# A graph network's first layer loads further ahead, scatters and copies later; its norms are regrouped

## The chip, the cores and the metric

The kernel runs on one core of a Trainium2 chip. The core has five engines that work side by side: TensorE (PE, matrix products and transposes; PEld is its weight load), VectorE (DVE), ScalarE (ACT), GpSimd (POOL) and SyncE (SP, which here only issues transfers). Sixteen DMA engines move data between DRAM and on-chip memory; a transfer is issued by an engine's queue, and gathers and scatters by index (DMA_INDIRECT) are all issued by POOL. The metric is the device time of one execution in microseconds (us); lower is better.

## The reference

A graph of N = 6250 nodes with 64 features (D) and 206250 edges, sorted by destination, each node with a loop edge to itself as its last one. Padded, there are 6272 nodes, 128 × 49.

```python
h = relu(layernorm(x))
msg  = relu(concat([h[dst], edge_attr_16]) @ W1 + b1)
aggr = segment_sum(msg, dst) / maximum(count, 1)
x = x + relu(aggr + h @ Wres + bres)           # layer 0
h = relu(layernorm(x))
for Wq, Wk, Wv, We, Ws, bq, bk, bv, bs, H in layers:     # three attention layers, 2, 2 and 1 heads
    kj = (h @ Wk + bk)[src] + edge_attr_32 @ We
    a  = segment_softmax(sum((h @ Wq + bq)[dst] * kj) / sqrt(C), dst)
    vj = (h @ Wv + bv)[src] + edge_attr_32 @ We
    h  = segment_sum(a * vj, dst) + h @ Ws + bs     # prelu after the first two
return x + h
```

## The kernel before

**Tiling.** Nodes are sorted by their number of edges and cut into NB = 49 blocks of 128, a node per partition; block b has room for CAP[b] edges a node (66, 46, 44, and so on down to 22), and every node in it has at least LEAST[b]. `full` tells, for the columns between LEAST and CAP, whether the node has such an edge. A block's work is then dense: partitions are nodes, columns are edges.

**Setup (L114 to L381).** The destinations are loaded in rows (`prev`, `cur`), x as `xs` (128 × 49 × 64), the sources `sf` are turned to the order of edges and written to DRAM as `srcs` (L222 to L236). A search (L184 to L271) finds each node's first edge and its count: a first pass over runs, seven gathers of the rows that matter (L213), `look_f` casts of them (L240), comparisons on DVE (L195) and on ACT (L200). A counting sort by count (L274 to L313, one-hot products) gives `at_i`, the first edge of each node in sorted order, and `num_i`, the node's number (L315 to L321). Beside this, x is normed in seven groups of LG = 7 blocks (L329 to L361): on DVE the mean (L336, L337), on POOL the subtraction (L339), on ACT the square, on DVE the variance (L343, L344), on ACT the root (L345), on DVE the reciprocal (L346), on POOL the product (L347), then PE transposes (L352), ACT's relu into `hT` (L355), and a product with `wn` (L358). POOL copies x beside it (L360), and SP writes rows of 192 numbers to the DRAM table `tabx` (L361): minus the message's part of the node, that part plus the residual product, and x itself. After at_i come `no`, `full` (41 instructions at L374) and `lack`, on DVE and POOL, which also check that the graph fits CAP and LEAST.

**Layer 0 (L461 to L617).** For block b, POOL gathers the node rows of tabx (`load_x`), the 16 edge features of all its edges (`load_e`, into a pool of four buffers), the sources (`load_src`) and the 32 edge features (`load_ea`), which SP then writes to the array `ean` for the attention. `load_src` is followed by an ACT copy of the block's last source column into `ends` (L490), for the check that the last edge of each node is its loop. `messages` (L499 to L540): PE transposes the features (`turn`, L508), ACT copies them (`eT`, L509), PE multiplies (`pm`, L518), DVE takes the maximum with the node's part into `msg` (L521, L531), multiplies the optional columns by `full`, and adds the columns up in a tree (L539). `finish` (L542 to L586) works on groups of FIN0 = 8, 8, 8, 8, 8, 4, 3 and 2 blocks: mean, residual, the norm of the new x (sum, subtraction, square, sum on DVE; the root on ACT, L570; reciprocal and product on DVE), transposes (L577), relu (`ht`, L579), the product with Wq, Wk, Wv, Ws (`po`, L584), and ACT's copy to `rows` (L586). `put` scatters a block's key and value rows to the DRAM table `tab` (L453).

**The order on POOL is written by hand** in that loop (L593 to L617); POOL issues one instruction after the other, and one that waits holds all behind it. Three blocks are loaded ahead; turn b issues `load_e(b + 3)`, a put, `load_x(b + 3)`, `load_src(b)`, a put, `load_ea(b)`. The puts are of a group whose last block is at least two turns back. The other engines' order comes from a scheduler that follows the same program.

**Loop check and attention.** After layer 0, L384 to L395 form `no_loop` from `ends` and sum the checks into `nbad_i`; an If (L397) on it chooses the attention (L620 to L758) or a general version that is not executed here. The attention fetches one indirect gather for each edge column of each block (`kv`, 4836 in three layers).

Of the kernel before, what the change touches and what calls it, by code (L numbers as in the profile page):

```python
# [97 lines left out]
def gnn_kernel(ctx: ExitStack, tc: tile.TileContext, x, src_t, dst_t, dst_row, ea16, ea32, eaT16, eaT32, w, out):  # L98
# [12 lines left out]
    bad = cp.tile([P, 5], F32, name="bad")  # L111
    k = ctx.enter_context(Kept(tc))

    with tc.tile_pool(name="chk", bufs=1) as p, tc.tile_pool(name="chk2", bufs=2) as p2, \  # L114
# [14 lines left out]
        nc.sync.dma_start(xs, x.rearrange("(p b) f -> p b f", b=NB))  # L129
        sf = p.tile([P, T], I32, name="sf")  # L130
# [20 lines left out]
        def iota(n, mult, pattern=None):  # L151
            i = p.tile([P, n], I32, name="iota_i", bufs=2)
            nc.gpsimd.iota(i, pattern=pattern or [[1, n]], base=0, channel_multiplier=mult)
            f = p.tile([P, n], F32, name=f"iota{n}_{mult}")
            nc.gpsimd.tensor_copy(f, i)
            return f
# [3 lines left out]
        col = iota(P, 0)  # L160
# [5 lines left out]
        cap = p.tile([P, NB], F32, name="cap")  # L166
        least = p.tile([P, NB], F32, name="least")
# [3 lines left out]
        nc.gpsimd.tensor_copy(cap, k.cap)  # L171
        nc.gpsimd.memset(cap[64:, 0:1], float(CAP0[64]))
        nc.gpsimd.memset(cap[32:64, 0:1], float(CAP0[32]))
# [9 lines left out]
        nc.vector.tensor_copy(first, prev.rearrange("w (c e) -> w c e", e=RUN)[:, :, 0])  # L183
        pb = pp.tile([P, WR, P], F32, name="pb")  # L184
# [26 lines left out]
        for g in range(NG0):  # L211
# [4 lines left out]
            got.append(t)  # L216

        nc.vector.memset(bad, 0.0)
        fall = p.tile([NW, WE], BF16, name="fall")
        nc.vector.tensor_tensor(fall, prev, cur, op=OP.is_gt)  # L220

# [16 lines left out]
        for g in range(NG0):  # L238
            f = p2.tile([P, LOOK], F32, name="look_f", bufs=3)
            (nc.gpsimd.tensor_copy if g else nc.scalar.copy)(f, got[g])  # L240
            for i in range(SG + (g == NG0 - 1)):
# [29 lines left out]
        nc.vector.tensor_scalar(cls, cls, -float(LOW), float(CLS - 1), op0=OP.add, op1=OP.min)  # L271

# [51 lines left out]

        wn = p.tile([D + 1, 2 * D], F32, name="wn")
        nc.gpsimd.tensor_scalar(wn[:, :D], w0[:, :D], -1.0, 0.0, op0=OP.mult, op1=OP.add)
        nc.gpsimd.tensor_add(wn[:, D:], w0[:, :D], w0[:, D:])
        LG = 7
        to_tab = tabx.rearrange("(p b) f -> p b f", b=NB)  # L329
        for g0 in range(0, NB, LG):  # L330
            g1 = g0 + LG
            n = LG
            rx = wp.tile([P, LG, 3 * D], F32, name="rx")
            xg = xs[:, g0:g1]
            m = wp.tile([P, LG], F32, name="ln_m")
            nc.vector.tensor_reduce(m[:, :n], xg, axis=AX.X, op=OP.add)  # L336
# [968 lines left out]
```

## Time and profile before

| | us |
|---|---|
| median of 3 runs (lowest, highest) | 6730.41 (6730.25, 6735.94) |
| profiled execution | 6732.95 |
| its span | 6731.2 |
| setup, until the first gather of layer 0 | 123.4 |
| layer 0, until the first gather of the attention | 454.3 |
| attention | 6153.5 |
| POOL, DVE, PE, ACT busy | 4927.7, 3127.9, 1914.8, 345.5 |

The span is cut at two of POOL's gathers: `e<-in_ea_dram,at_i` for the first block, and the first `kv<-tab,src`. In a timeline row, what stands in brackets is the idle time of the engine before that instruction and what ended it. A row of the waits is engine, line, what was waited for, total us, number of times, longest. Engines wait for each other by semaphores, and the profile infers from these what released an instruction. An engine that is idle but isn't the one that ends a stage costs nothing.

### The profile page before, as it was taken

To read this page: it belongs to the slowest core of one execution; us is meant where nothing else is said; L and a number is where in the kernel's file an instruction comes from. 1 tells how busy PE (TensorE), PEld (TensorE's weight loads), DVE (VectorE), ACT (ScalarE), POOL (GpSimd) and SP (SyncE) were. 2 spreads that over 40 slices of the span, in tenths; PEclk is the share of its full clock that TensorE was granted. 3 is DMA by queue.
4 is the path that set the end of the run, shared out by engine and by line. 5 is a ranking of instruction groups with operands and counts; after the bars stand their busy time and mean duration, and the time that the engine had idled before them with its cause. 6 is when DMAs were issued, how large, how long until landed. Compare 5 with 4: busy or idle time off the path is not lost. (4 is left out here: it accounts for less than half of the span.)

```text
span 6731.2 us, 26890 instructions
## 1 busy us (share of the span) xinstructions
PE 1914.8 (28%) x4808; PEld 1135.6 (17%) x4808; DVE 3127.9 (46%) x5986; ACT 345.5 (5%) x998; POOL 4927.7 (73%) x5264
## 2 busy tenths in 40 slices
PE   4663232333333332222222222222222222222221
PEld 3442111111111111111111111111111111111110
DVE  7763444444444444444444444444444344444444
ACT  3110000000000000000000000000000000000000
POOL 4556777777777776777777777776777777777776
PEclk9765555555555555555555555555555555555555
DMA  4553232333232322222222222222222222222221
GB/s 144 183 175 122 81 87 79 84 84 84 82 87 81 84 82 60 67 69 66 68 69 68 68 70 67 69 68 64 64 63 68 63 66 66 66 64 67 63 65 55
DMA packets 227799, 535.37 MB, mean 80 GB/s; under 512 B 90199, under 2 KB 106685, under 8 KB 226519
## 3 DMA queue, kind: packets, MB, share of 16 engines
q0 software_dynamic: 172736, 374.78, 19.6%
q1 hardware_dynamic: 52790, 156.27, 7.0%
q10 hardware_dynamic: 2090, 2.48, 0.1%
q14 instruction: 142, 1.16, 0.1%
q8 instruction: 41, 0.67, 0.0%
HBM read 459.32 MB, written 73.87 MB: 79 GB/s over the span
## 5 line engine op out<-in xcount | busy, mean ns | idle before, releaser
L447 POOL DMA_INDIRECT kv<-tab,src x4836 | 4561.7, 943 | 1518.6 <-issue 1410.4
L688 DVE TENSOR_TENSOR kv<-kv,pe 128x1024 f32<-128x1024 f32 (+6 forms) x669 | 745.0, 1114 | 2321.1 <-DMA kv<-tab,src 2152.6
L682 PE MATMUL pe<-wblk,ea 128*128 128x256 f32 x1736 | 901.4, 669 | 3046.8 <-DVE kv L688 2747.1
L682 PEld LDWEIGHTS pe<-wblk,ea 128*128 128x128 f32 x1736 | 505.7, 323 | 3420.6 <-DVE kv L688 2967.0
L682 PE MATMUL pe<-wblk,eaT 128*128 128x256 f32 x868 | 451.4, 668 | 1224.9 <-DVE kv L688 1160.8
L721 DVE TENSOR_REDUCE some<-kv 128x64 f32<-128x512 f32 (+6 forms) x690 | 610.6, 922 | 0.1
L687 DVE CAST src<-kv 128x8 int32<-128x8 f32 (+5 forms) x223 | 41.0, 184 | 1092.5 <-DMA kv<-tab,src 1041.6
L682 PEld LDWEIGHTS pe<-wblk,eaT 128*128 128x128 f32 x868 | 252.1, 322 | 1383.1 <-DVE kv L688 1273.3
L694 DVE TENSOR_TENSOR prod<-kv,more 128x512 f32<-128x512 f32 (+6 forms) x690 | 423.7, 628 | 0.8
L695 DVE TENSOR_REDUCE al<-prod 128x16 f32<-128x512 f32 (+8 forms) x690 | 422.9, 627 | 0.7
L717 DVE TENSOR_TENSOR kv<-kv,more 128x512 f32<-128x512 f32 (+6 forms) x690 | 416.7, 627 | 0.0
L706 ACT ACTIVATE more<-al,m 128x33 f32<-128x33 f32 (+22 forms) x245 | 71.7, 293 | 3189.0 <-DVE m L704 3185.8
L518 PE MATMUL pm<-w0blk,eT 64*128 64x256 f32 x868 | 192.2, 564 | 37.0 <-DVE msg L521 20.0
L659 PE MATMUL turn<-ident,ea 128*128 128x128 f32 x434 | 124.9, 432 | 77.5 <-ACT eaT L660 70.8
L453 POOL DMA_INDIRECT tab<-rows,num_i x49 | 54.5, 1112 | 117.5 <-ACT rows L586 97.9
L539 DVE TENSOR_TENSOR msg<-msg 128x960 f32<-128x960 f32 (+19 forms) x224 | 137.4, 617 | 0.8
L518 PEld LDWEIGHTS pm<-w0blk,eT 64*128 64x128 f32 x868 | 120.3, 276 | 89.6 <-DVE msg L521 25.7
L521 DVE TENSOR_TENSOR msg<-pm,rx 128x1024 f32<-128x1024 f32 x76 | 92.8, 1221 | 77.4 <-PE pm L518 72.0
L447 POOL DMA_INDIRECT e<-in_ea_dram,at_i x98 | 103.8, 1059 | 33.8 <-issue 22.2
L738 PE MATMUL po<-ws,ht 65*128 65x256 f32 x196 | 109.2, 661 | 11.5 <-ACT ht L736 11.5
L674 ACT COPY more<-rows 128x64 f32<-128x64 f32 x147 | 31.6, 216 | 1516.3 <-DVE kv L717 1507.9
L659 PEld LDWEIGHTS turn<-ident,ea 128*128 128x128 f32 x434 | 80.2, 217 | 139.1 <-ACT eaT L660 125.9
(183 smaller groups left out, 1442.8 us busy)
## 6 DMA issues: line engine op xcount, KB each, us to landing
kv<-tab,src POOLq DMA_INDIRECT x4836, 2.5
ea<-eat SPq DMA_DIRECT2D x26, 576.0 KB
ea<-eat SPq DMA_DIRECT2D x24, 512.0 KB
ea<-eat SPq DMA_DIRECT2D x16, 640.0 KB
ean<-e SPq DMA_DIRECT2D x13, 576.0 KB
ea<-ean SPq DMA_DIRECT2D x13, 576.0 KB
eat<-eaT SPq DMA_DIRECT2D x13, 576.0 KB
ea<-eat SPq DMA_DIRECT2D x16, 448.0 KB
```

What stands on the lines that cost most here:

```text
L447: return nc.gpsimd.indirect_dma_start(out=out, out_offset=None, in_=table, in_offset=bass.IndirectOffsetOnAxis(ap=idx, axis=0))
L518: nc.tensor.matmul(pm[:, r, u].rearrange("p j f -> p (j f)"), eT[h, t0 // 8 + u, :], k.w0blk[h, :], start=True, stop=True)
L521: nc.vector.tensor_tensor(msg[:, t0:t0 + 16], pm.rearrange("p r u j f -> p (r u j) f"), nega[:, None, :].to_broadcast([P, 16, D]), op=OP.max)
L539: nc.vector.tensor_add(to, msg[:, :h], msg[:, c - h:c])
L659: nc.tensor.transpose(ps[:, i - i0, :], t[:, i, :], ident)
L682: nc.tensor.matmul(pe[:, 4 * g:4 * g + 4].rearrange("p j f -> p (j f)"), ea[:, t0 // 4 + g, :], k.wblk[l], start=True, stop=True)
L688: nc.vector.tensor_add(pair(kv[:, :m, :2 * D]), pair(kv[:, :m, :2 * D]), pe[:, :m, None, :].to_broadcast([P, m, 2, D]))
L694: nc.vector.tensor_mul(prod[:, :n], kv[:, :n, :D], q[:, None, :].to_broadcast([P, n, D]))
L695: nc.vector.tensor_reduce(al[:, :H, t0:t0 + n].rearrange("p h j -> p j h"), prod[:, :n].rearrange("p j (h c) -> p j h c", h=H), axis=AX.X, ...
L717: nc.vector.tensor_mul(v.rearrange("p j (h c) -> p j h c", h=H), v.rearrange("p j (h c) -> p j h c", h=H), ex[:, :H, t0:t0 + n].rearrange( ...
L721: nc.vector.tensor_reduce(some[:, i, :], v.rearrange("p j f -> p f j"), axis=AX.X, op=OP.add)
L738: nc.tensor.matmul(po, ht[:, :P], k.ws[l + 1], start=True, stop=True)
```

## The change

- **x into tabx.** A DMA issued by POOL ahead of everything else copies x straight into the last 64 columns of tabx; the tile `rx` of the setup then holds 128 columns, and SP writes pieces of 512 B a row, in groups of eight blocks instead of seven.
- **The norm of x in whole passes.** One mean reduce over all of x on DVE, before the counts; four subtractions on POOL and four squares on ACT; one variance reduce on DVE, one root on ACT, one reciprocal; six products on POOL, which stand between the `look_f` casts. Transposes, relu and product follow the comparisons on ACT, before the counting sort. `k.ht` is used for the relu.
- **Moved.** The reduce of `fall` and the copies of weights to `ws` come earlier in the setup. `no`, `full` and `lack` leave the setup for the head of layer 0, and are all on DVE; the tile `cap` goes, and two comparisons for the narrower lanes of block 0 take its place.
- **Order in layer 0.** AHEAD: `load_e` and `load_x` run four blocks ahead, not three; e16 has five buffers and one of its own for block 0, e32 three and one of its own. LATE: puts are of groups at least four turns back, and the copies to `ends` (now `last`) of block b − 4 follow the gather of block b. LATER: `load_ea` is for block b − 6. The remaining copies, six `load_ea` and the last puts come after the loop, a `load_ea` with up to two puts.
- **messages.** Where at most three columns are optional, they are left out of the tree and added to the sum by multiply-add with their column of `full`.
- **finish.** The norm's subtraction, square and sum on DVE go. ACT squares each block with the mean as bias and sums it up in the same instruction, eight for a group; DVE forms (x + m) · v block by block. `h0` has one buffer, `sq` two.

```diff
         nc.sync.dma_start(xs, x.rearrange("(p b) f -> p b f", b=NB))
+        nc.gpsimd.dma_start(tabx[:, 2 * D:], x)
         sf = p.tile([P, T], I32, name="sf")
...
-        cap = p.tile([P, NB], F32, name="cap")
         for t, values in ((k.cap, CAP), (least, LEAST)):
...
                 nc.gpsimd.memset(t[:, i:j], float(v))
-        nc.gpsimd.tensor_copy(cap, k.cap)
-        nc.gpsimd.memset(cap[64:, 0:1], float(CAP0[64]))
-        nc.gpsimd.memset(cap[32:64, 0:1], float(CAP0[32]))
         going = p.tile([P, CLS, NB], BF16, name="going")
...
         nc.vector.tensor_copy(first, prev.rearrange("w (c e) -> w c e", e=RUN)[:, :, 0])
+        mean = p.tile([P, NB], F32, name="mean")
+        var = p.tile([P, NB], F32, name="var")
+        hn = p.tile([P, NB, D], F32, name="hn")
+        sq = k.rows.rearrange("p b f -> p (b f)")[:, 2 * WE + NG0 * LOOK:2 * WE + NG0 * LOOK + NB * D] \
+            .rearrange("p (b f) -> p b f", f=D)
+        part4 = [slice(0, 13), slice(13, 25), slice(25, 37), slice(37, 49)]
+        nc.vector.tensor_reduce(mean, xs, axis=AX.X, op=OP.add)
+        nc.vector.tensor_scalar(mean, mean, 1.0 / D, None, op0=OP.mult)
+        for s in part4:
+            nc.gpsimd.tensor_sub(hn[:, s], xs[:, s], mean[:, s, None].to_broadcast([P, s.stop - s.start, D]))
+            nc.scalar.activation(sq[:, s], hn[:, s], AF.Square)
         pb = pp.tile([P, WR, P], F32, name="pb")
...
             got.append(t)
+        nc.vector.tensor_reduce(var, sq, axis=AX.X, op=OP.add)
+        nc.vector.tensor_scalar(var, var, 1.0 / D, 1e-5, op0=OP.mult, op1=OP.add)
+        nc.scalar.activation(var, var, AF.Sqrt)
+        nc.vector.reciprocal(var, var)
...
         nc.vector.tensor_tensor(fall, prev, cur, op=OP.is_gt)
+        nc.vector.tensor_reduce(bad[:NW, 0:1], fall, axis=AX.X, op=OP.max)
...
             (nc.gpsimd.tensor_copy if g else nc.scalar.copy)(f, got[g])
+            if g:
+                s = slice(8 * (g - 1), min(NB, 8 * g)) if g < 6 else slice(40, NB)
+                nc.gpsimd.tensor_mul(hn[:, s], hn[:, s], var[:, s, None].to_broadcast([P, s.stop - s.start, D]))
             for i in range(SG + (g == NG0 - 1)):
...
         nc.vector.tensor_scalar(cls, cls, -float(LOW), float(CLS - 1), op0=OP.add, op1=OP.min)
+        wn = p.tile([D + 1, 2 * D], F32, name="wn")
+        nc.gpsimd.tensor_scalar(wn[:, :D], w0[:, :D], -1.0, 0.0, op0=OP.mult, op1=OP.add)
+        nc.gpsimd.tensor_add(wn[:, D:], w0[:, :D], w0[:, D:])
+        for t in k.ht:
+            nc.gpsimd.memset(t[D:D + 1, :], 1.0)
+        LG = 8
+        to_tab = tabx.rearrange("(p b) f -> p b f", b=NB)
+        for g0 in range(0, NB, LG):
+            g1 = min(NB, g0 + LG)
+            rx = wp.tile([P, LG, 2 * D], F32, name="rx")
+            for b0 in range(g0, g1, 4):
+                nb = min(4, g1 - b0)
+                pt = psum.tile([D, 4 * P], F32, name="pr_t")
+                for b in range(nb):
+                    nc.tensor.transpose(pt[:, b * P:(b + 1) * P], hn[:, b0 + b, :], ident)
+                ht = k.ht[b0 // 4 % 2]
+                nc.scalar.activation(ht[:D, :nb * P], pt[:, :nb * P], AF.Relu)
+                po = psum.tile([P, 4, 2 * D], F32, name="pr_o")
+                for b in range(nb):
+                    nc.tensor.matmul(po[:, b, :], ht[:, b * P:(b + 1) * P], wn, start=True, stop=True)
+                nc.scalar.copy(rx[:, b0 - g0:b0 - g0 + nb], po[:, :nb])
+            nc.sync.dma_start(to_tab[:, g0:g1, :2 * D], rx[:, :g1 - g0])
+        for l in range(LAYERS):
+            nc.gpsimd.tensor_copy(k.ws[l][:, :D], wl[l][:, 3 * D:])
+            nc.gpsimd.tensor_scalar(k.ws[l][:, D:2 * D], wl[l][:, :D], float(D // HEADS[l]) ** -0.5, 0.0, op0=OP.mult,
+                                    op1=OP.add)
+            nc.gpsimd.tensor_copy(k.ws[l][:, 2 * D:], wl[l][:, D:3 * D])
...
-        LG = 7
...
-            rx = wp.tile([P, LG, 3 * D], F32, name="rx")
-            xg = xs[:, g0:g1]
-            m = wp.tile([P, LG], F32, name="ln_m")
-            nc.vector.tensor_reduce(m[:, :n], xg, axis=AX.X, op=OP.add)
-            nc.vector.tensor_scalar(m[:, :n], m[:, :n], 1.0 / D, None, op0=OP.mult)
-            hn = wp.tile([P, LG, D], F32, name="hn0")
-            nc.gpsimd.tensor_sub(hn[:, :n], xg, m[:, :n, None].to_broadcast([P, n, D]))
-            sq = wp.tile([P, LG, D], F32, name="ln_sq")
-            nc.scalar.activation(sq[:, :n], hn[:, :n], AF.Square)
-            v = wp.tile([P, LG], F32, name="ln_v")
-            nc.vector.tensor_reduce(v[:, :n], sq[:, :n], axis=AX.X, op=OP.add)
-            nc.vector.tensor_scalar(v[:, :n], v[:, :n], 1.0 / D, 1e-5, op0=OP.mult, op1=OP.add)
-            nc.scalar.activation(v[:, :n], v[:, :n], AF.Sqrt)
-            nc.vector.reciprocal(v[:, :n], v[:, :n])
-            nc.gpsimd.tensor_mul(hn[:, :n], hn[:, :n], v[:, :n, None].to_broadcast([P, n, D]))
...
-            nc.gpsimd.tensor_copy(rx[:, :, 2 * D:], xg)
-            nc.sync.dma_start(to_tab[:, g0:g1], rx)
         nc.gpsimd.tensor_copy(k.rows[:, :, 4 * D:4 * D + 1], place[:, :, None])
...
-        nc.vector.tensor_reduce(bad[:NW, 0:1], fall, axis=AX.X, op=OP.max)
-        no = p.tile([P, 2, NB], F32, name="no")
-        nc.vector.tensor_tensor(no[:, 0], k.deg, cap, op=OP.is_gt)
-        nc.vector.tensor_tensor(no[:, 1], k.deg, least, op=OP.is_lt)
-        nc.vector.tensor_reduce(bad[:, 1:3], no, axis=AX.X, op=OP.add)
-        for b in range(NB):
-            if CAP[b] > LEAST[b]:
-                s = slice(WOFF[b], WOFF[b + 1])
-                nc.vector.tensor_scalar(k.full[:, s], col[:, LEAST[b]:CAP[b]], k.deg[:, b:b + 1], None, op0=OP.is_lt)
-        nc.gpsimd.tensor_scalar(k.lack, k.full, BIG, -BIG, op0=OP.mult, op1=OP.add)
...
-    layer0(tc, ea16, ea32, ident, tabx, srcs, k)
+    layer0(tc, ea16, ea32, ident, tabx, srcs, k, col, least, bad)
     with tc.tile_pool(name="nb", bufs=1) as p, tc.tile_pool(name="nbp", bufs=1, space=PSUM) as pp:
...
-def layer0(tc, ea16, ea32, ident, tabx, srcs, k):
+def layer0(tc, ea16, ea32, ident, tabx, srcs, k, col, least, bad):
     nc = tc.nc
...
         nc.vector.memset(eps, 1e-5)
-        for t in k.ht:
-            nc.vector.memset(t[D:D + 1, :], 1.0)
+        no = wp.tile([P, 2, NB], F32, name="no", bufs=1)
+        nc.vector.tensor_tensor(no[:, 0], k.deg, k.cap, op=OP.is_gt)
+        nc.vector.tensor_tensor(no[:, 1], k.deg, least, op=OP.is_lt)
+        nc.vector.tensor_single_scalar(no[64:, 0, 0:1], k.deg[64:, 0:1], float(CAP0[64]), op=OP.is_gt)
+        nc.vector.tensor_single_scalar(no[32:64, 0, 0:1], k.deg[32:64, 0:1], float(CAP0[32]), op=OP.is_gt)
+        nc.vector.tensor_reduce(bad[:, 1:3], no, axis=AX.X, op=OP.add)
+        for b in range(NB):
+            if CAP[b] > LEAST[b]:
+                s = slice(WOFF[b], WOFF[b + 1])
+                nc.vector.tensor_scalar(k.full[:, s], col[:, LEAST[b]:CAP[b]], k.deg[:, b:b + 1], None, op0=OP.is_lt)
+        nc.vector.tensor_scalar(k.lack, k.full, BIG, -BIG, op0=OP.mult, op1=OP.add)
         st = {}
...
             n = up(CAP[b], 8)
-            t = st["e16", b] = gp.tile([P, up(MAXC, 8) * 16], F32, name="e16")
+            t = st["e16", b] = gp.tile([P, n * 16], F32, name="e16_0", bufs=1) if b == 0 else \
+                gp.tile([P, up(CAP[1], 8) * 16], F32, name="e16", bufs=5)
             pick(nc, t[:, :n * 16], ea16, k.at_i[:, b:b + 1])
...
             pick(nc, k.src[0][:, OFF[b]:OFF[b + 1]], srcs[:, None], k.at_i[:, b:b + 1])
+        def last(b):
             nc.scalar.copy(k.ends[:, b:b + 1], k.src[0][:, OFF[b + 1] - 1:OFF[b + 1]])
...
             at = k.at_i[:, b:b + 1]
-            t = gp.tile([P, max(G32) * P], F32, name="e32", bufs=3)
+            t = gp.tile([P, G32[0] * P], F32, name="e32_0", bufs=1) if b == 0 else \
+                gp.tile([P, G32[1] * P], F32, name="e32", bufs=3)
             pick(nc, t[:, :G32[b] * P], ea32, at)
...
                                                 nega[:, None, :].to_broadcast([P, m, D]), op=OP.max)
-            if c > LEAST[b]:
+            few = range(LEAST[b], c) if c - LEAST[b] <= 3 else ()
+            if c > LEAST[b] and not few:
                 nc.vector.tensor_mul(msg[:, LEAST[b]:c], msg[:, LEAST[b]:c],
                                      k.full[:, WOFF[b]:WOFF[b + 1], None].to_broadcast([P, c - LEAST[b], D]))
+            sum_ = st["sum", g][:, b - first[g]:b - first[g] + 1, :]
+            c -= len(few)
             while c > 1:
                 h = c // 2
-                to = msg[:, :h] if c > 2 else st["sum", g][:, b - first[g]:b - first[g] + 1, :]
-                nc.vector.tensor_add(to, msg[:, :h], msg[:, c - h:c])
+                nc.vector.tensor_add(msg[:, :h] if c > 2 else sum_, msg[:, :h], msg[:, c - h:c])
                 c -= h
+            for i, j in enumerate(few):
+                w = WOFF[b] + i
+                nc.vector.scalar_tensor_tensor(sum_, msg[:, j:j + 1], k.full[:, w:w + 1], sum_, op0=OP.mult, op1=OP.add)
...
             nc.vector.reciprocal(c[:, :n], c[:, :n])
-            h = wp.tile([P, GN, D], F32, name="h0")
+            h = wp.tile([P, GN, D], F32, name="h0", bufs=1)
             nc.vector.tensor_mul(h[:, :n], s[:, :n], wide(c))
...
             nc.vector.tensor_reduce(m[:, :n], x, axis=AX.X, op=OP.add)
-            nc.vector.tensor_scalar(m[:, :n], m[:, :n], 1.0 / D, None, op0=OP.mult)
-            nc.vector.tensor_sub(h[:, :n], x, wide(m))
-            sq = wp.tile([P, GN, D], F32, name="sq", bufs=1)
-            nc.vector.tensor_mul(sq[:, :n], h[:, :n], h[:, :n])
+            nc.vector.tensor_scalar(m[:, :n], m[:, :n], -1.0 / D, None, op0=OP.mult)
             v = wp.tile([P, GN], F32, name="v0")
-            nc.vector.tensor_reduce(v[:, :n], sq[:, :n], axis=AX.X, op=OP.add)
+            for i in range(n):
+                sq = wp.tile([P, D], F32, name="sq")
+                nc.scalar.activation(sq, x[:, i], AF.Square, bias=m[:, i:i + 1], accum_out=v[:, i:i + 1])
             nc.scalar.activation(v[:, :n], v[:, :n], AF.Sqrt, bias=eps[:, 0:1], scale=1.0 / D)
             nc.vector.reciprocal(v[:, :n], v[:, :n])
-            nc.vector.tensor_mul(h[:, :n], h[:, :n], wide(v))
+            for i in range(n):
+                nc.vector.tensor_scalar(h[:, i], x[:, i], m[:, i:i + 1], v[:, i:i + 1], op0=OP.add, op1=OP.mult)
             for i0 in range(0, n, 4):
...
         wait = []
+        AHEAD, LATE, LATER = 4, 4, 6
         with tc.manual_schedule(engines={mybir.EngineType.Pool}):
-            for b in range(3):
+            for b in range(AHEAD):
                 load_e(b)
...
             for b in range(NB):
-                old = [r for r, at in wait if at <= b - 2][:2]
+                old = [r for r, at in wait if at <= b - LATE][:2]
                 wait = wait[len(old):]
-                if b + 3 < NB:
-                    load_e(b + 3)
+                if b + AHEAD < NB:
+                    load_e(b + AHEAD)
                 if old:
                     put(old.pop(0))
-                if b + 3 < NB:
-                    load_x(b + 3)
+                if b + AHEAD < NB:
+                    load_x(b + AHEAD)
                 load_src(b)
...
                     put(old.pop(0))
-                load_ea(b)
+                if b >= LATER:
+                    load_ea(b - LATER)
+                if b >= LATE:
+                    last(b - LATE)
                 messages(b)
...
                     wait += [(r, b) for r in range(first[g], first[g] + FIN0[g])]
-        for r, _ in wait:
-            put(r)
+            for b in range(NB - LATE, NB):
+                last(b)
+            rest = list(range(NB - LATER, NB))
+            while rest or wait:
+                if rest:
+                    load_ea(rest.pop(0))
+                for r, _ in wait[:2]:
+                    put(r)
+                wait = wait[2:]
```

## The prediction

> **What bounds the kernel now.** I read the windows by stage first: the setup until block 0's edge gather is issued (123.4), layer 0 until the first attention gather (577.7), and the attention. After the two bounds come duration, busy time of PE, PEld, DVE, ACT and POOL (instruction counts in brackets), granted clock, DMA share and GB/s.
>
> ```profile
> 0.00:123.40 123.40, 51.56 (x229) 42.60 (x229) 95.41 (x212) 48.83 (x110) 50.74 (x134) 1.00 0.31 98
> 123.40:577.70 454.30, 289.74 (x1247) 184.03 (x1247) 303.10 (x615) 65.17 (x175) 265.49 (x245) 0.69 0.54 180
> 577.70:6731.20 6153.50, 1573.47 (x3332) 908.97 (x3332) 2729.41 (x5159) 231.54 (x714) 4611.43 (x4885) 0.51 0.25 72
> ```
>
> The attention is 91% of the span. Its groups say that POOL issues 4836 gathers, each 943 ns with some 300 ns ("issue" idle) after it: 4836 × 1.24 = 6011 us. None of its code is edited, so the 6153.5 us stay; the change can move only the first 577.7. Next, the waits of layer 0 (window 123 to 572: total us, times, longest):
>
> ```profile
> ACT ends L490 <- DMA src<-srcs,at_i: 197.0, 41, 8.9
> POOL tab L453 <- ACT rows L586: 97.9, 6, 29.5
> DVE msg L521 <- PE pm L518: 72.0, 32, 6.2
> ```
>
> ACT stands 197 us on the loop-check copies (L490), and POOL, which issues every gather of the stage, 97.9 us on six table scatters (L453). POOL's timeline shows where: start, duration, and in brackets the idle time before and its releaser.
>
> ```profile
> 123.44 1.02 POOL L447 DMA_INDIRECT e<-in_ea_dram,at_i  x1 [1.52 <-PE pr_o L358]
> 127.90 0.95 POOL L447 DMA_INDIRECT rx<-tabx,num_i  x1 [3.45 <-DMA tabx<-rx]
> 221.72 1.03 POOL L453 DMA_INDIRECT tab<-rows,num_i  x1 [29.51 <-ACT rows L586]
> 295.51 1.02 POOL L453 DMA_INDIRECT tab<-rows,num_i  x1 [18.08 <-ACT rows L586]
> ...
> 499.10 1.15 POOL L453 DMA_INDIRECT tab<-rows,num_i  x1 [9.28 <-ACT rows L586]
> ...
> 577.77 0.99 POOL L447 DMA_INDIRECT kv<-tab,src  x1 [6.00 <-issue]
> ```
>
> Each row with L586 is the first scatter of a group of eight blocks. The group's last ACT copy is late, POOL stands, no gather is issued, and the next blocks start late. The groups between have stalls of 17.27 and 14.04. DVE's timeline gives the setup's end:
>
> ```profile
> 113.22 0.20 DVE L316 SCALAR_TENSOR_TENSOR at_i<-join 128x49 int32<-128x49 f32 x1
> ...
> 115.64 5.83 DVE L374 TENSOR_SCALAR full<-iota,deg 128x22 f32<-128x22 f32 x41
> ```
>
> The list that gathers need (at_i) is there at 113.4, but the first gather is issued at 123.44, and block 0's rows of tabx come at 127.90.
>
> **The setup.** DVE's rows L336, L343 and the small ones of norm run between the counts and the permutation. From 60 to 113 I add five L343 reduces (0.62 each, the profile's row at 112.69) and three L336 (0.62): 5.0, some 1.5 of small rows of 0.16 to 0.2, and waits for POOL and ACT of about 1.2. DVE's rows beside POOL's norm work run long there too (L309, val, is 1.58 to 2.31 for one form; three such stretches give some 3): about 9.5 leave. One whole reduce is added before the counts. By 7 pieces at the pitch of a pair of the L336 rows (1.14 for two, so 0.57) it is 4.0, against pieces that filled gaps there: the counts end 1.5 later, with POOL's four subtractions (7 × 0.92 by L339 = 6.4) before the seven gathers at 27.9. Net, at_i comes 8 earlier (bounds 4 and 11).
>
> Behind at_i, POOL now waits for pr_o (L358), for `lack`, and for tabx. Norm's product ends long before, `full` (5.83) and `lack` stand at the head of layer 0 on DVE, and there the first e and x gathers cover them (first gather 123.44, first message 133.77: 10.3). So e(0) follows at_i by 1.7 (num_i, num, one queue step) instead of 10.1: −8.4. x(0), the one that was issued last, gains the 3.45 wait as well, but the DVE needs block 0's e and x together. I take −8 −8.4 = −16.4, bounds −9 to −23 (all of 127.90 − 105).
>
> **The copy of x into tabx** is one DMA on POOL, ahead of all its setup: 6272 rows of 256 B, DRAM to DRAM. No row of this trace has POOL issue a plain DMA, so I bound it by the indirect ones:
>
> ```profile
> 636.52 0.94 POOL L447 DMA_INDIRECT kv<-tab,src  x1 [0.30 <-issue]
> 641.37 0.87 POOL L447 DMA_INDIRECT kv<-tab,src  x1 [0.30 <-issue]
> ```
>
> The second gather writes 32 lanes, the first 128: 0.07 more for 96 more rows, 0.73 ns per row. So 6272 rows are 0.87 + 4.5 = 5.4 us at the one end, and 49 × 0.94 = 46 us at the other, if every 128 rows cost a whole issue. POOL's setup before the data arrive is busy 6.4 in 2 to 18, so 5.4 is covered by the 10 us that it idles until x lands at 18.4; 46 is not: the seven run gathers go from 29.7 to 61, +31. I take 5.4, as the rows within one instruction are the nearer likeness to one instruction.
>
> What it moves competes: in 2 to 18 the DMA engines are 94% busy. In 658 to 700 the share is 0.22 of 16 engines for 34 gathers of 128 rows, so a row of 528 B takes 0.22 × 16 × 42 / 4352 = 34 ns, and 6272 rows are 213 us on one engine, 13.3 on sixteen. x (18.4) shares the engines with it and lands between 0 and 13.3 later. I take +8, somewhat past the middle because the copy and the rows it delays are issued at the same time; all of the setup behind moves with it.
>
> A rule speaks against the copy: the Trainium skill, page "DMA: Bandwidth & Descriptors", section Specifications, says that a transfer of at least 512 B is the minimum for line rate, and that below it the engine reads, modifies and writes. No trace here shows rows of 256 B beside rows of 512 B. By that rule a 256-B row could cost up to twice the 34 ns that the gathers' row shows, an estimate from that page: 27 us of all engines, and the whole sum would stand near −26 instead of −45.
>
> **Layer 0, group 0** (blocks 0 to 7). From the first message (133.77) to the first scatter (221.72) are 88 us. DVE is busy 60.25 of the 71.8 between 133.7 and 205.5, and the stall of 29.51 on POOL covers the group's finish. ACT no longer holds block b's transposed copies (eT) behind block b's own src gather: the copy `ends` moves four blocks behind. With its 11.5 idle halved to gone, DVE ends the group 6 to 11.5 earlier, and a fourth block ahead changes nothing here because DVE, not the gathers, sets it. The finish keeps its length (below). I take −11, bounds 0 and −15.
>
> **Groups 1 to 4.** The distance between first scatters is 73.8, 71.3, 68.5 and 63.7, sum 277.3; each holds 40 issues on POOL (8 each of e, x, src, ea and put) in 54.4 to 55.7, so 1.36 apiece with their gaps, and a stall of 18.1, 17.3, 14.0 or 9.3. In the new order the put of a group stands four blocks behind its last block, not two. But it does not follow that the stall vanishes: the finish's squares are now ACT instructions, eight a group, and in ACT's order they stand behind eT(b+3) and the ends copy of b+3's turn, as the square root stood behind eT(b+4) before. They come with e(b+3) landed, and the first put is only two POOL issues behind that turn's. From the issue that ACT waits for I count: landing 3.0 (2.5 from the src issue at 136.65 to the copy at 139.17, and a little for busier queues), copy 0.2, eT 0.85 (L509), eight squares of 64 columns at 0.35 = 3 (an L490 copy of one column is 0.19, L570 0.30; bounds 1.6 to 3.3), root 0.3 (L570), root to last needed rows 6.3 (215.16 to 221.44, L570 to L586); sum 13.6, less three issues of 1.36 that POOL does meanwhile: 9.6 stall. A cycle is then 40 × 1.36 + 9.6 = 64, four are 257: −20 against 277.3. The bounds are a stall of 18 left (0) and none (−58.7 for the four stalls).
>
> Finish on DVE gives up a subtraction, a product and a reduce (0.68 each for 8 blocks) and takes eight `tensor_scalar` of 64 columns for the product. That is −2 + 1 on an engine that waits; zero, with ±1 per group. `few` replaces a product over up to three columns per block by up to three multiply-adds of 64: three at 0.2 against one at 0.25 to 0.35; ±0.2 × 49 = ±10 on DVE, covered by its waits of 72 us for PE (L521) in groups 1 to 7; without that cover up to +10.
>
> **The tail.** From group 4's first put to the first attention gather are 577.77 − 499.10 = 78.7. It loses the stalls 9.75 and 6.78 in part, and the six late e32 gathers come last: e(48) of them is the last issue, lands in 4, its copy to `ean` on SP takes about 2.5, and the check follows (573.57 to 577.77, 4.2, L387, unchanged). SP's `ean` copies, moved six blocks later, wait behind nothing else on SP's queue. I count 73.4: −5, bounds −15 and +5.
>
> **Sum.** −16.4 + 8 − 11 − 20 − 5 = −44.4, say −45 against the profiled execution's 6732.95, which stands 2.5 above the median of 6730.41: 6688, in terms of the median **6686**.
>
> **Rivals.** *A, POOL needs 46 us to issue the copy.* For it: each indirect issue costs 0.94. Against: the 32-lane rows. +31.6 while the +8 of the engines is then hidden: −45 + 23 = −22, 6708. *B, the puts stop waiting.* For it: four blocks is twice two. Against: ACT's order above. The remaining 38 of the four stalls go, and 10 of the tail: 6638. *C, slower:* the issue of the copy holds POOL for over 67 us (10.7 ns a row; the seven gathers then start behind it, and every us more is a us of span). At that price the gain of 45 is used up, at 85 us the time is 6748. Against: no row is over 7.3 ns a row. *D, the stalls only move:* landing of src and squares keep the 18, the engines' share takes the 8; setup −8, no more: 6722, within 0.2%.
>
> **How the numbers follow.** Forecast 0.62, A 0.16, B 0.13, D 0.05, C 0.04. A measurement of this kernel can tell about 0.2%, 13.5 us, from no change. Faster: forecast, A and B, less a little: 0.90; same 0.05; slower 0.05. The forecast alone, with setup and engine bounds, spans 6655 to 6705. The range takes in B at the low end and A at the high one: 6635 to 6712; C and D lie outside.
>
> **What would show it.** The copy's row on POOL (5.4, or 46); x landing (18.4 now) near 26; e(0) issued near 107 + 8; at the first put of groups 1 to 4 stalls near 10, released by ACT rows, or "issue" if B holds; the L490 wait far under 197; the first attention gather near 533. I am wrong if POOL's copy is long, if the attention moves at all, or if the stalls are other than 10.

## The result and the profile after

The changed kernel takes 6717.29 us (median of 13 runs, 6703.75 to 6722.09) against 6733.19 for the kernel before (13 runs, 6729.21 to 6735.94): a ratio of 0.9975 with a 95% interval of 0.9967 to 0.9984, some 16 us. The prediction was 6686, a gain of 44, with a range up to 6712. The direction is right, the size is not.

The profiled execution took 6718.75 us with a span of 6717.0, so 14.2 less than the one shown of before. Its windows by stage, cut at the same two gathers (columns as in the table of before):

```profile
0.00:112.20 112.20, 50.14 (x229) 42.67 (x229) 85.08 (x142) 47.35 (x99) 36.14 (x108) 1.00 0.38 114
112.20:557.80 445.60, 273.63 (x1247) 173.21 (x1247) 304.17 (x679) 80.81 (x272) 268.19 (x245) 0.71 0.55 183
557.80:6717.00 6159.20, 1569.33 (x3332) 906.67 (x3332) 2729.78 (x5159) 231.54 (x714) 4611.85 (x4885) 0.51 0.25 72
```

The setup is 11.2 shorter, layer 0 only 8.7, and the attention, none of whose code is edited, is 5.7 longer. The waits of layer 0 (window 112 to 553) tell why so little came of the new order:

```profile
ACT ends L496 <- DMA src<-srcs,at_i: 227.5, 45, 9.2
PEld turn L515 <- ACT eT L516: 93.9, 28, 11.4
PE turn L515 <- ACT eT L516: 81.8, 24, 10.7
DVE msg L528 <- PE pm L525: 68.5, 26, 10.4
POOL tab L446 <- ACT rows L598: 61.1, 7, 17.8
```

ACT's wait for src at the loop-check copy, which was to go, grew from 197.0 to 227.5 us. POOL's wait at the scatters fell by more than a third, from 97.9 to 61.1. POOL's timeline has the copy of x, the first gather of layer 0 and the first scatters of groups 1 to 4 (group 0's, at 206.78, is left out):

```profile
1.35 2.33 POOL L132 DMA_DIRECT2D tabx<-in_x_dram  x1 [0.82 <-POOLq L1298]
...
112.24 1.01 POOL L440 DMA_INDIRECT e<-in_ea_dram,at_i  x1 [0.91 <-DVE no L466]
...
280.49 1.01 POOL L446 DMA_INDIRECT tab<-rows,num_i  x1 [17.76 <-ACT rows L598]
...
346.91 1.01 POOL L446 DMA_INDIRECT tab<-rows,num_i  x1 [11.03 <-ACT rows L598]
...
411.80 1.01 POOL L446 DMA_INDIRECT tab<-rows,num_i  x1 [7.36 <-ACT rows L598]
...
476.22 1.01 POOL L446 DMA_INDIRECT tab<-rows,num_i  x1 [9.01 <-ACT rows L598]
```

DVE's timeline shows when x has landed, in the kernel before and in the changed one, and when the changed kernel has at_i:

```profile
18.41 1.14 DVE L336 TENSOR_REDUCE ln_m<-x 128x7 f32<-128x448 f32 x2 [0.77 <-DMA x<-in_x_dram]
```

```profile
19.78 3.42 DVE L189 TENSOR_REDUCE mean<-x 128x49 f32<-128x3136 f32 x1 [2.31 <-DMA x<-in_x_dram]
...
110.49 0.21 DVE L365 SCALAR_TENSOR_TENSOR at_i<-join 128x49 int32<-128x49 f32 x1
```

And a stretch of ACT's timeline in group 1 shows what its 227.5 us stand in front of:

```profile
221.78 0.19 ACT L496 CAST ends<-src 128x1 f32<-128x1 int32 x1 [5.47 <-DMA src<-srcs,at_i]
221.88 0.74 ACT L516 COPY eT<-turn 128x512 f32<-128x512 f32 x2
229.38 0.19 ACT L496 CAST ends<-src 128x1 f32<-128x1 int32 x1 [6.76 <-DMA src<-srcs,at_i]
229.48 0.74 ACT L516 COPY eT<-turn 128x512 f32<-128x512 f32 x2
```

In the program the copy to ends is that of a block four turns back, whose sources landed long ago. In ACT's stream it is that of the newest block: the copy at 221.78 is the thirteenth, and it stands right behind the thirteenth gather of src, issued at 217.10, while the fourteenth is issued only at 226.86. The order on ACT is the scheduler's, not the program's; by what rule it moved the copies up, no run shows. Here the copy then waits 5 to 7 us for a gather of src, and the block's eT copy, whose input is there, starts 0.1 us after it. So the new line "four blocks late" changed nothing on the engine where it was to act.

Where the 14.2 us came from, by stretches between the same events in the two profiled executions:

| stretch | before | after | difference | predicted |
|---|---|---|---|---|
| start to first gather of e | 123.44 | 112.24 | −11.2 | −8.4 |
| to group 0's first scatter | 98.3 | 94.5 | −3.7 | −11 |
| first scatters of group 0 to group 4 | 277.4 | 269.4 | −7.9 | −20 |
| to the attention's first gather (tail) | 78.7 | 81.6 | +2.9 | −5 |
| the attention's first eight gathers | 10.1 | 12.9 | +2.9 | 0 |
| to the output's last scatter | 6137.84 | 6137.81 | 0 | 0 |
| to the span's end | 5.5 | 8.4 | +2.9 | 0 |

### The profile page after: what moved, and what is told of

The parts are those of the page before. It is cut to its first block, busy times and chain, and to the rows that moved or that the text cites. A ratio compares the mean times of both kernels' runs of the same rounds, so it can differ in the third digit from the quotient of the medians.

```text
span 6717.0 us, 26905 instructions
## 1 busy us (share of the span) xinstructions
PE 1893.1 (28%) x4808; PEld 1122.5 (17%) x4808; DVE 3119.0 (46%) x5979; ACT 359.7 (5%) x1085; POOL 4916.2 (73%) x5238
## 3 DMA queue, kind: packets, MB, share of 16 engines
q0 software_dynamic: 173152, 376.39, 19.8%
## 5 line engine op out<-in xcount | busy, mean ns | idle before, releaser
L548 DVE TENSOR_TENSOR msg<-msg 128x128 f32<-128x128 f32 (+12 forms) x221 | 134.0, 610 | 1.0
L528 DVE TENSOR_TENSOR msg<-pm,rx 128x1024 f32<-128x1024 f32 x76 | 92.6, 1221 | 68.7 <-PE pm L525 68.5
L446 POOL DMA_INDIRECT tab<-rows,num_i x49 | 53.9, 1101 | 88.8 <-ACT rows L598 61.1
```

What stands on the lines that cost most here:

```text
L528: nc.vector.tensor_tensor(msg[:, t0:t0 + 16], pm.rearrange("p r u j f -> p (r u j) f"), nega[:, None, :].to_broadcast([P, 16, D]), op=OP.max)
L548: nc.vector.tensor_add(msg[:, :h] if c > 2 else sum_, msg[:, :h], msg[:, c - h:c])
```

## Experiments

All runs keep the whole computation. Times are medians, and a ratio is to the kernel before run beside that kernel, which took 6732 to 6734 unless said otherwise. "Group 0" is the stretch from the first gather of e to group 0's first scatter, and the "distances" are those between the first scatters of groups 0 to 4: 94.5 and 73.7, 66.4, 64.9, 64.4 in the changed kernel, 98.3 and 73.8, 71.3, 68.5, 63.7 before.

**The copies to ends, really late.** An order edge on ACT, without a semaphore, puts the copy of block b behind the eT copies of block b + 4; the call of last moves behind messages.

```diff
-            nc.scalar.copy(k.ends[:, b:b + 1], k.src[0][:, OFF[b + 1] - 1:OFF[b + 1]])
+            i = nc.scalar.copy(k.ends[:, b:b + 1], k.src[0][:, OFF[b + 1] - 1:OFF[b + 1]])
+            tc.add_manual_dep(i.ins, st["eT", min(NB - 1, b + 4)].ins.name,
+                              mybir.DependencyInfo(mybir.DependencyClass.NoSync, mybir.DependencyReason.DATA),
+                              reason="copies of ends behind eT of four blocks on")
```

> The changed kernel, with each copy to ends (last) put behind the eT copies of four blocks later in ACT's own order, where the scheduler had moved it up to the newest gather of src. Theory 1, ACT's wait for src holds eT and with it the groups: the L496 wait falls from 227.5 us to under 60, group 0 (first gather of e to first scatter, 94.5) shortens to about 88, group 1 (73.7) to about 66, and the time stands some 15 us under the changed kernel's, near 6702. Rival, DVE and the gathers of e set the groups and ACT's wait only fills idle time: the wait goes to turn and eT, every distance between first scatters stays within 2 us, the time stays within 5 us of the changed kernel's 6717.

Measured: 6671.93 us, ratio 0.9909 (0.9893 to 0.9926), 45 under the changed kernel. Its waits at these two places, and the first scatters of groups 1 to 4:

```profile
POOL tab L446 <- ACT rows L601: 24.3, 7, 6.7
...
ACT ends L496 <- DMA src<-srcs,at_i: 6.2, 1, 6.2
```

```profile
258.62 1.01 POOL L446 DMA_INDIRECT tab<-rows,num_i  x1 [6.67 <-ACT rows L601]
...
315.79 1.11 POOL L446 DMA_INDIRECT tab<-rows,num_i  x1 [1.55 <-ACT rows L601]
...
375.94 1.01 POOL L446 DMA_INDIRECT tab<-rows,num_i  x1 [1.18 <-ACT rows L601]
...
433.08 1.01 POOL L446 DMA_INDIRECT tab<-rows,num_i  x1 [2.89 <-ACT rows L601]
```

ACT's wait for src falls from 227.5 to 6.2, POOL's stalls from 17.8, 11.0, 7.4 and 9.0 to 6.7, 1.6, 1.2 and 2.9. Group 0 takes 85.1, the distances are 62.5, 57.2, 60.1 and 57.1, and the attention's first gather comes at 509.9 instead of 557.8. Theory 1 holds, and by three times what it expected; its rival falls. This one order of 49 small copies is worth more than the whole change had given.

**The gathers of ea in their own turn.**

```diff
-        AHEAD, LATE, LATER = 4, 4, 6
+        AHEAD, LATE, LATER = 4, 4, 0
```

> The changed kernel with LATER = 0: each gather of ea in its own block's turn, none left for the end. Theory 2, the gathers of ea left for the end cost the tail what the groups gained: the stretch from the last group's first scatter (535.3) to the attention's first gather (557.8), 22.5 us, shortens to about 10, and the time to about 6705. Rival, the work only moves back into the groups, where the transfers to ean compete with the gathers: the tail is shorter by 12, the five full groups longer by 10 to 12 together, and the time stays within 4 us of 6717.

Measured: 6699.70 us, ratio 0.9950 (0.9933 to 0.9967). First the changed kernel's tail on POOL and the first instruction of the check on DVE, then the tail of this run on POOL:

```profile
529.79 0.99 POOL L440 DMA_INDIRECT e<-in_ea_dram,at_i  x1 [0.30 <-issue]
...
535.30 0.98 POOL L446 DMA_INDIRECT tab<-rows,num_i  x1 [3.21 <-ACT rows L598]
536.58 0.99 POOL L440 DMA_INDIRECT e<-in_ea_dram,at_i  x1 [0.30 <-issue]
...
545.80 0.94 POOL L440 DMA_INDIRECT e<-in_ea_dram,at_i  x1 [4.36 <-DMA ean<-e]
557.82 0.94 POOL L440 DMA_INDIRECT kv<-tab,src  x1 [11.08 <-issue]
```

```profile
553.08 0.21 DVE L380 TENSOR_TENSOR no_loop<-ends,num 128x49 f32<-128x49 f32 x1 [21.69 <-DMA ean<-e]
```

```profile
538.17 0.98 POOL L446 DMA_INDIRECT tab<-rows,num_i  x1 [6.45 <-ACT more L696]
539.46 0.98 POOL L446 DMA_INDIRECT tab<-rows,num_i  x1 [0.30 <-issue]
542.62 0.99 POOL L440 DMA_INDIRECT kv<-tab,src  x1 [2.18 <-PE turn L681]
```

In the changed kernel the gathers of ea that were left stand between scatters that wait for the last groups' finish, the last of them waits 4.4 for a free buffer, and the check waits until its copy to ean has landed. With them gone, the stretch from the last group's first scatter to the attention's first gather is 4.5 instead of 22.5, while the distances (75.1, 67.8, 62.7, 64.2) together stay within 0.5 of the changed kernel's. Theory 2 holds, its rival falls.

**Both edits.**

> The changed kernel with both edits: copies to ends really four blocks late on ACT, and LATER = 0. If the two losses are separate they add up: the groups as with the late copies alone (85, 62, 57, 60, 57), the stretch from the last group's first scatter to the attention's first gather 4.5 instead of 22.9, time near 6672 - 18 = 6654. Rival, without the wait for src the groups have no idle time in which gathers of ea and the copies to ean fit: each group is longer by 3 to 4, time near 6668.

Measured: 6651.56 us, ratio 0.9877 (0.9860 to 0.9893): group 0 85.2, distances 61.1, 56.9, 59.9 and 56.6, tail stretch 4.5. The two losses are separate and add up; the rival falls.

**The parts alone.** First the kernel before with all of the change's setup (with `no`, `full` and `lack` at the head of layer 0), then the kernel before with all of its layer 0; of each, two lines of the diff stand for the whole.

```diff
+        nc.gpsimd.dma_start(tabx[:, 2 * D:], x)
...
+        nc.vector.tensor_reduce(mean, xs, axis=AX.X, op=OP.add)
```

> The kernel before with the changes of the setup alone (copy of x by POOL, norm in whole passes, the checks at the head of layer 0), layer 0's order and finish as before. If the parts add up: first gather of e at 112 (123.4 before), layer 0 from there as before, 454, time 11 us under the kernel before, near 6722. Rival, the earlier start is given back in group 0, where ACT and DVE are the limit: first gather at 112 but the attention's first gather still near 575, time within 4 us of the kernel before.

```diff
+        AHEAD, LATE, LATER = 4, 4, 6
...
+                nc.scalar.activation(sq, x[:, i], AF.Square, bias=m[:, i:i + 1], accum_out=v[:, i:i + 1])
```

> The kernel before with the changes of layer 0 alone (four ahead, scatters four and gathers of ea six turns back, squares on ACT, optional columns added after the tree), the setup as before. If the parts add up: layer 0 shortens from 454 to 446, time 5 to 9 us under the kernel before, near 6726. Rival, the layer's order needs the earlier start or brings nothing by itself: time within 3 us of the kernel before or above it.

Measured: the setup alone 6728.86 (0.9995, 0.9985 to 1.0005), layer 0 alone 6722.31 (0.9985, 0.9976 to 0.9995). Layer 0 alone is 10 under the kernel before, a little more than the 5 to 9 expected, and 444.2 long. The setup alone is 3.4 under, not clear of no change, so the 11 expected did not come, and the rival's time (within 4) did; but its reason did not. The setup alone brought the attention's first gather from 577.77 to 564.82, 13 earlier, so the early start is not given back in group 0, as the rival had it. It is given back later: the first eight gathers of the attention take 12.9 instead of 10.1, and from the output's last scatter to the span's end are 8.4 instead of 5.5. In the run with layer 0 alone these are 10.0 and 4.5.

**The copy of x issued by SP instead of POOL.**

```diff
-        nc.gpsimd.dma_start(tabx[:, 2 * D:], x)
+        nc.sync.dma_start(tabx[:, 2 * D:], x)
```

> The changed kernel with the copy of x into tabx issued by SP, behind the load of x, instead of by POOL. In the changed kernel, and in the setup's change alone, the attention's first eight gathers take 12.9 us (10.1 before), and from the last scatter of the output to the span's end are 8.4 us (5.5 before). Theory 3, both come with a plain copy in POOL's queue: they return to 10.1 and 5.5, time near 6717 - 6 = 6711. Rival, they come with the setup's other edits or the moved instructions: both stay, and the time is within 3 us of 6717, apart from what x's landing (19.8) gains or loses.

Measured: 6707.40 us, ratio 0.9958 (0.9944 to 0.9972), 10 under the changed kernel. The attention's second and third gather, in the changed kernel and in this run:

```profile
559.45 0.94 POOL L440 DMA_INDIRECT kv<-tab,src  x1 [0.69 <-issue]
561.08 0.94 POOL L440 DMA_INDIRECT kv<-tab,src  x1 [0.69 <-DMA tab<-rows,num_i]
```

```profile
556.05 0.94 POOL L440 DMA_INDIRECT kv<-tab,src  x1 [0.30 <-issue]
557.30 0.94 POOL L440 DMA_INDIRECT kv<-tab,src  x1 [0.30 <-issue]
```

When x has landed in this run:

```profile
18.36 3.42 DVE L189 TENSOR_REDUCE mean<-x 128x49 f32<-128x3136 f32 x1 [0.64 <-DMA x<-in_x_dram]
```

The eight gathers take 10.0 again, the end 4.6. Theory 3 holds: both losses follow the queue that the copy is issued from. What in POOL's queue makes them, the profile does not show, and it stays open. Of the 10.7 that the span is shorter than the changed kernel's, 3.0 lie before the attention's first gather: x lands at 18.4 as in the kernel before, and at_i is ready at 109.7, 1.0 earlier than in the changed kernel.

**The late copies on the kernel before.** The order edge of the first run, put on the kernel before; nothing else.

```diff
+            tc.add_manual_dep(i.ins, st["eT", min(NB - 1, b + 4)].ins.name,
...
+                if b >= 4:
+                    last(b - 4)
```

> The kernel before with one edit: the copies to ends behind the eT copies of four blocks later in ACT's own order; three ahead, scatters two turns back, gathers of ea in their own turn, setup and finish as before. Theory 1: ACT's L490 wait (197 us) goes, the six stalls of POOL at the first scatters (97.9 us) shrink by a third or more, and the time falls by 25 or more, below 6707, which is more than the whole change gave. Rival, four turns for the scatters are needed as well: the stalls of 14 to 18 stay, and the time is within 8 us of 6732.

Measured: 6722.25 us, ratio 0.9985 (0.9975 to 0.9994). ACT's wait for src falls from 197.0 to 9.7 here too, and group 0 shortens from 98.3 to 87.1. But the scatters stand only two turns back, and POOL stalls at them as before (groups 1 to 3):

```profile
284.66 1.02 POOL L453 DMA_INDIRECT tab<-rows,num_i  x1 [15.94 <-ACT rows L591]
...
356.00 1.02 POOL L453 DMA_INDIRECT tab<-rows,num_i  x1 [16.99 <-ACT rows L591]
...
424.59 1.02 POOL L453 DMA_INDIRECT tab<-rows,num_i  x1 [14.04 <-ACT rows L591]
```

Theory 1 as it was expected here falls: the distances are 73.9, 71.3, 68.6 and 63.7, within 0.1 of before. The late copies bring 11 in group 0 and nothing in the others. The rival has the stalls right, and its time (within 8 of 6732) just missed. The late copies alone bring little, then, and so did the rest of the new order without them; the last runs split further which part of it they need.

**The norm of finish on DVE again,** on top of both edits (the squares are written into a column range of rx that is free by then).

```diff
-            for i in range(n):
-                sq = wp.tile([P, D], F32, name="sq")
-                nc.scalar.activation(sq, x[:, i], AF.Square, bias=m[:, i:i + 1], accum_out=v[:, i:i + 1])
+            nc.vector.tensor_sub(h[:, :n], x, wide(m))
+            sq = rx[:, :, D:2 * D]
+            nc.vector.tensor_mul(sq[:, :n], h[:, :n], h[:, :n])
+            nc.vector.tensor_reduce(v[:, :n], sq[:, :n], axis=AX.X, op=OP.add)
```

> As the run with both edits (late copies to ends, LATER = 0), but finish's norm on DVE as in the kernel before: subtraction, square, sum and one product of all blocks, no squares on ACT. Eight squares with their reads took 2.8 us on ACT in the changed kernel, the three instructions on DVE about 2.0. If the finish is on nobody's path once POOL no longer waits: within 3 us of the run with both edits, in either direction. If the stall at the first scatter still ends with ACT: 3 to 6 us faster. If DVE sets group 0 and 1: 3 to 6 us slower.

Measured: 6650.73 us, 0.9871 (0.9855 to 0.9888), no different from 6651.56. That is what was expected if the finish is on nobody's path, but not for that reason: group 0 is 1.9 longer (87.1), the distances (56.2, 56.7, 57.7, 59.4) are 4.6 shorter in sum, and the stretch from group 4's first scatter to the attention's first gather is 2.5 longer (61.9 for 59.4). The parts cancel.

**Two turns back, three ahead, and the best version.** Four kernels were first run where the kernel before itself took 7687.58 us; in the profiles of the four, layer 0's groups and the attention are longer (the attention's middle 7042 to 7047 for 6137). Their numbers (7597.56 for both edits with SP's copy, 7627.76 for the same with the norm on DVE, 7666.07 for two turns, 7644.29 for three ahead) can't be set beside the others. Among themselves two turns and three ahead lose there too, by more than SP's copy is worth, but the norm on DVE is 30 us slower in the median than the squares on ACT. The same four were run again where the kernel before took 6733.28.

```diff
-        AHEAD, LATE, LATER = 4, 4, 0
+        AHEAD, LATE, LATER = 4, 2, 0
```

> Late copies to ends, LATER = 0, copy of x by POOL, scatters two turns back. Theory 4: stalls of 14 to 17 at the first scatters of groups 1 to 4 and a time near 6690. Rival, four blocks ahead carry the groups over the stalls: time under 6672.

```diff
-        AHEAD, LATE, LATER = 4, 4, 0
+        AHEAD, LATE, LATER = 3, 4, 0
```

> Late copies to ends, LATER = 0, copy of x by POOL, three blocks ahead, scatters four turns back. If the scatters' turns are what counts: within 5 us of 6651.6. Rival, turn waits for e without the fourth block: above 6667.

Measured: scatters two turns back 6690.84 (0.9937, 0.9921 to 0.9954), three blocks ahead 6666.23 (0.9902, 0.9886 to 0.9919), against 6651.56 with four and four. With two turns the time is theory 4's 6690, and its rival (under 6672) falls. The stalls are back, though at 9 to 11 and not the 14 to 17 expected; of groups 1 to 3:

```profile
265.34 1.01 POOL L446 DMA_INDIRECT tab<-rows,num_i  x1 [11.28 <-ACT rows L601]
...
329.01 1.01 POOL L446 DMA_INDIRECT tab<-rows,num_i  x1 [9.16 <-ACT rows L601]
...
393.93 1.01 POOL L446 DMA_INDIRECT tab<-rows,num_i  x1 [11.25 <-ACT rows L601]
```

With three ahead, the stalls at the first scatters of groups 3 and 4 (1.3 and 1.2 with four):

```profile
380.99 1.01 POOL L446 DMA_INDIRECT tab<-rows,num_i  x1 [6.75 <-ACT rows L601]
...
443.27 1.01 POOL L446 DMA_INDIRECT tab<-rows,num_i  x1 [7.71 <-ACT rows L601]
```

With ACT's order mended and the other in place, the scatters' turns are worth 39 us and the fourth block 15. With the scheduler's order, all of layer 0's change together took only 8.5 from the four distances (the run with layer 0 alone). The scatters' turns do not explain everything either: with two turns and four blocks ahead the distances sum to 260.5, with the late copies on the kernel before, which has two turns and three ahead and the old finish, to 277.6. The 15 us of the fourth block lie mostly in the third and fourth distance (65.2 and 62.3 for 59.9 and 56.6), that is, in the two stalls above. Neither expectation fits: the time is 14.7 above where the scatters' view allowed 5, and the rival's wait of turn for e hardly grew (41.3 for 37.0 in all of layer 0), its 6667 just missed.

> Late copies to ends, LATER = 0 and the copy of x issued by SP, on a chip where the kernel before takes its 6732. If the loss from POOL's plain copy is separate: 6643, group 0 85 and groups 1 to 4 near 61, 57, 60, 57. Rival: within 3 us of 6651.6.

> As the first of these, finish's norm on DVE as in the kernel before: within 3 us of it if the finish is on nobody's path; more than 3 slower if the squares on ACT are worth something.

Measured: both edits with SP's copy 6646.28 (0.9870, 0.9854 to 0.9887), and with the norm on DVE besides 6642.65 (0.9866, 0.9849 to 0.9882). With SP's copy the attention's first eight gathers take 10.1 and the end 4.5, so that loss is separate from layer 0, and the rival (within 3 us of 6651.6) falls. The gain, 5.3, is 3 short of the 6643 expected: in the profiles the attention's two stretches are 6.8 shorter, but its first gather comes 3.0 later (493.3 for 490.2), by a cause that was not looked for. The four runs of the first are 6643.99 to 6647.71, of the second 6641.91 to 6643.37: the squares on ACT cost some 3.6 there, more than the 3 that were to tell the two readings apart. Since they were 30 better beside the kernel of 7687.58, which form is to be preferred stays open. The last is the fastest kernel of this study, 90 us under the kernel before and 75 under the changed one.

## Why the prediction was wrong, step by step

**The bound** was read rightly. The attention's middle stayed as it was (6137.84 and 6137.81 between the same events), and only what lies before it, and the attention's two ends, moved.

**The setup** came out better in sum, −11.2 for −8.4, by luck: two terms were mis-sized and nearly cancel. Up to at_i I had −8 for norm's work out of DVE and +8 for the copy, 0 together; it was −2.7 (at_i ready at 110.7 for 113.4). The run with SP's copy splits that: at_i is ready 1.0 earlier there, so the copy on POOL cost 1.0, not 8, and norm's move brought 3.7, not 8. POOL issued the copy in 2.33 us (5.4 predicted; rivals A and C, 46 and over 67, are gone), and x landed at 19.8, 1.4 later. The counts end 1.3 later (1.5 predicted), but from there to at_i the gain is 4.0 where I had 9.5 (and the terms that I listed for it add up to 10.7): DVE's wait for PE's `pperm`, 2.6 before, is 6.8. The gather behind at_i is −8.5, as predicted −8.4.

From the Trainium skill's page "DMA: Bandwidth & Descriptors", section Specifications, which gives 512 B as the least transfer for line rate, I had estimated up to 27 us of engine time for the copy. No run here has the same copy in pieces of 512 B; what the profile shows is that x, which the copy could have delayed, came 1.4 late, so neither that estimate nor my 13.3 reached the path.

**Group 0** is the step that failed first: "ACT no longer holds block b's transposed copies (eT) behind block b's own src gather". It was read from the program's text, which the scheduler was taken to follow, while the order on ACT is the scheduler's own. ACT's wait grew to 227.5, and the stretch lost 3.7 where I had 11. With the copies really late it loses 9.4 more on the changed kernel, and 11.2 on the kernel before: the mechanism and its size were right, the change did not do it.

**Groups 1 to 4.** The wait for the finish behind a gather of src that I had kept in the sum was there: stalls of 17.8, 11.0, 7.4 and 9.0 against 9.6 each, and distances that sum to 269.4 for my 257 (four cycles of 64 are 256). Of the 12 missing, 6.8 are in the stalls, group 1's alone being 8 too long; the rest lies between the stalls, 56.1 a group for my 54.4. What I had not asked is whether it must be so: rival B (no stalls, −38 more) was given 0.13 on the ground of ACT's order. With that order mended the kernel goes about half the way to B: the distances sum to 237.0, and 12.3 of stalls are left.

**The tail,** −5 predicted, was +2.9. I had let "SP's `ean` copies, moved six blocks later, wait behind nothing else" and counted only the last gather's landing. The six gathers stand in POOL's queue between scatters that wait for the last finishes, and three buffers make the last one wait for SP's copies. Layer 0's own work ended earlier, last group's first scatter 535.3 against 569.5, and 18 us of that were lost here: the gain was made and given back. The second run shows it by taking the delay away.

**The attention at 0** missed +5.8, three at its start and three at the end, by a cause that is shown as far as the queue: a plain copy issued by POOL.

**The squares on ACT** were priced rightly (eight take 2.8 us for 3 predicted). With ACT's order mended, moving them back to DVE changed the time by nothing, or by −3.6.

The sum of misses, 2.8 to the good and 7.3, 12.1, 7.9 and 5.8 to the bad, makes the 30 between −44.4 and −14.2. The measured time is nearest to rival D's 6722, but that is chance: D kept every stall at 18 and gave 8 to the engines' share of the copy, which were 11.3 on average and 1.0.

## What to carry to other kernels

Before a move is priced, find out in which order the engine that it is to help will run it: a line placed late in the program is not late if a scheduler may pull it up, and a copy of 0.2 us that waits 5 to 7 us at the head of an engine's stream holds all that stands behind it. Work that is put off to the end of a loop needs a place there, so name what it stands behind and what waits for it; and when moves pay only together, price and measure each with the others in place: the late copies brought 12 us on the kernel before and 45 on the changed one.

## What the runs showed that was not expected

One plain copy of 6272 rows on POOL's queue, at 1.35 us of the span, is followed some 490 us later or more by 0.64 to 0.77 us after each of the attention's first seven gathers instead of 0.30, and by 2.9 to 4 us more at the very end. It shows in all ten profiles with the copy on POOL and in none of the five with the copy on SP; no profile shows the cause.
